# A routed mixture-of-experts layer: row numbers written by ScalarE, other banks for turned x, and the second tile's rows turned behind layer 2 of the first

## The chip, the cores and the metric

One core of one Trainium2 chip runs the whole kernel. The metric is the device time of one execution in microseconds (us); below, a time "at 24.77" is counted from the start of the profiled span.

The engines are PE (TensorE, with PEld for its weight loads), DVE (VectorE), ACT (ScalarE), POOL (GpSimd) and SP (which here only issues DMAs). Each works through its own queue in order. PE writes only to PSUM, which has eight banks, PB[0] to PB[7] in the code; ACT and DVE copy from there to SBUF.

## What is computed

Each of 4096 tokens (64 x 64) has 256 features. A gate, computed on the normalised token plus a term from its condition vector, picks 2 of 8 experts; every expert is a three-layer perceptron, and the two outputs are added to the token with the softmax weights of the two.

```
var = mean(x * x); xn = rms_w * (x * rsqrt(var + EPS))
gate = xn @ wg_W + wg_b + (cond @ gg_W + gg_b);  gate_w = softmax(gate)
topk_w, topk_i = top_k(gate_w, 2);  cw = one_hot(topk_i) weighted by topk_w, summed
h1 = relu(x @ W1[e] + b1[e]);  h2 = relu(h1 @ W2[e] + b2[e])
out = x + sum over e of cw[e] * (h2 @ W3[e] + b3[e])
```

W1 is 256 x 512, W2 512 x 512 and W3 512 x 256 for each expert, all in fp32.

## The kernel before

The kernel computes only the chosen experts. A **tile** is 128 tokens of one expert. Its rows are gathered from DRAM by an indirect DMA of POOL (`gather`, L719), turned by PE and copied by ACT into xT (`transpose_x`, L746), and taken through layer1 (L816), layer2 (L829) and layer3 (L846); then DVE scales the sum and POOL adds it into the output rows by another indirect DMA (`give`, L855). For each of the four column blocks of layer1 and layer2, PE accumulates into bank PB[0], PB[1], PB[2] or PB[3], and ACT applies the relu behind it.

The order within each engine is written out by hand: the whole body is under a manual schedule, so an engine's queue is the program's order of calls.

**The head of the program.** The first eight tiles, one of each expert, hold tokens of a first part of x alone (8 of the 32 rows of each partition), so that they can start before the rest has been routed.

- `first_part` (L398) loads x, squares it (`squares`, L180), turns it by PE (`turn_pe`, L192), copies it out of a bank (`turn_copy`, L202, by DVE or ACT; the row of the profile is L205 or L207), multiplies with the gate matrix (`gates_2`, L220; `gates`, L209), sets the result upright (`upright_2`, L227), chooses the experts (class `Part`, `choose`, L295), ranks the tokens, and finds the token of every slot of the first tiles by comparing row numbers with ranks (L477 to L481). The row numbers, `iotx`, are 128 numbers, each 16 times over, in fp16; POOL writes them with one iota at L417.
- `second_part` (L508) goes on with the rest of x beside the first gather: five more groups are turned, three of them here. `turn(j, c, n, eng, bank)` says which engine copies, and which bank of the list TB, that is PB[0], PB[1], PB[2], PB[5], PB[4], holds the turned group. PB[0] and PB[1] are also banks of layer1. `transpose_x(0)` is among these calls.
- `third_part` (L527) stands behind layer1 of tile 0: the last group is turned, the remaining squares follow on DVE, a first set of gates is set upright, and the gates of the last two groups are computed into PB[7] and copied by ACT into gTs.
- `last_upright` (L536) sets those last gates upright from gTs (eight matmuls, L231) into PB[6], and ACT copies them into graw, which the routing of the rest (`rest`, L549, a generator that hands DVE work out between the tiles) reads on DVE at L299. `rest` also reuses the memory of gTs from L555 on.
- `head_step` (L888) orders one of the first tiles. For tile 0, layer2 is called with functions that it calls in between (L907): after its second column block `last_upright`, after its third `transpose_x(1)`, the rows of the second tile. So the order on PE is blocks 0 and 1, the last upright gates, block 2, the rows of tile 1, block 3; on ACT it is the relus of blocks 0 and 1, the copy of the gates, the relu of block 2, the copy of xT, the relu of block 3.

After the first eight tiles come pairs of tiles and single tiles, in which PE has work without a break. The weights of all experts are loaded once, by DMAs that SP issues in one long row (`other_loads`, L489).

Of the kernel before, what the change touches and what calls it, by code (L numbers as in the profile page):

```python
# [21 lines left out]
def kernel(  # L22
# [17 lines left out]
    nc = tc.nc  # L40
# [40 lines left out]
    def buf(pool, shape, name, dt=F32):  # L81
        return pool.tile(shape, dt, tag=name, name=name)
# [91 lines left out]
    graw = t3("graw", NI)  # L174
    gTs = buf(gx, [P, TPB * P], "gTs")
    ohA = buf(gx, [P, P, GC], "hotA", F16)
    sqs = {"A": buf(gx, [P, H], "sqA", F16), "V": buf(gx, [P, H], "sqV", F16)}
    TB = [PB[k] for k in (0, 1, 2, 5, 4)]

# [7 lines left out]
    def turn(j, c, n, eng, bank):  # L187

        turn_pe(j, c, bank)
        turn_copy(n, eng, bank)  # L190
# [36 lines left out]
    def upright_2(dst):  # L227

        gtp = dst[:, 0 : TPB * P // 2].rearrange("p (k r) -> p k r", k=TPB)
        for k in range(TPB):  # L230
            nc.tensor.matmul(gtp[:, k], lhsT=gTs[:, ts(k, P)], rhs=both, start=True, stop=True)  # L231
        return gtp.rearrange("p k (q e) -> p q k e", q=2)[:, :, :, 0:E]

    def upright():

        gtp = PB[4].rearrange("p (k r) -> p k r", k=TPB)
        for k in range(TPB):
            nc.tensor.transpose(gtp[:, k], gTs[:, ts(k, P)], ident)
        return gtp.rearrange("p k (q e) -> p q k e", q=TPB)[:, :, :, 0:E]

    def busy(n):

# [155 lines left out]
    def first_part():  # L398


        rw2 = gTs[0:HC, 0:P]
        load_x(0)
        nc.scalar.dma_start(wg_in, wg_W.rearrange("(c p) e -> p c e", p=P))
        load_x(1)
        nc.scalar.dma_start(rw2, rms_w.rearrange("(c p) -> c p", c=HC))
        load_x(2, 2)
        nc.scalar.dma_start(gg_sb[0:G, :], gg_W)
        load_x(4, 2)
        nc.scalar.sqrt(warm, ones[:, 0:E])
        V.memset(wg_sb, 0.0)  # L410
        V.memset(condT[G : G + 2, :, :], 1.0)
        V.memset(cw8B, 0.0)
        for k in range(3):
            V.memset(ring(run, [P, H], "xg", 3, k), 0.0)
        V.memset(cgR, 0.0)
        nc.gpsimd.dma_start(cwdA.rearrange("(p i) e -> p i e", p=P)[:, NA:NI, :], cw8B[:, NA:NI, :])
        nc.gpsimd.iota(iotx, [[1, P], [0, GC]], base=0, channel_multiplier=0, allow_small_or_imprecise_dtypes=True)  # L417
        busy(7)
        rwp, cps, gps = PB[7][:, P : P + HC], PB[7][0:G, 2 * P : 2 * P + B], PB[7][:, 3 * P : 3 * P + E]
        nc.tensor.transpose(rwp, rw2, ident[:HC, :HC])  # L420
        V.tensor_copy(rwT, rwp)
        for c in range(HC):
            V.tensor_scalar(wg_sb[:, c, 0:E], wg_in[:, c, :], rwT[:, c : c + 1], None, ALU.mult)
        for i in (2, 3):
            squares(i, "A")
        turn(0, 0, 0, "V", 0)
        turn(0, 1, 1, "A", 1)
        squares(0, "V")
        turn(1, 0, 2, "V", 2)
        squares(TPB + 2, "A")  # L430
        turn(1, 1, 3, "A", 3)
        squares(TPB + 3, "A")
        nc.tensor.transpose(cps, cond_sb, ident[:B, :B])
        for i in (1, TPB, TPB + 1):
            squares(i, "V")
        V.tensor_copy(condT[0:G], cps.unsqueeze(2).to_broadcast([G, B, REP]))
        for j in range(NG - GA, NG):
            load_x(j)
        nc.sync.dma_start(vecs[0 : E * MC, :], b1.rearrange("e (c p) -> (e c) p", p=P))
        nc.sync.dma_start(vecs[E * MC : 2 * E * MC, :], b2.rearrange("e (c p) -> (e c) p", p=P))  # L440
        load_weights(0, (0, 1))
        gates_2(((0, 1), (2, 3)), PB[3])
        nc.scalar.copy(gTs, PB[3])
        pA.norm(True)
        turn(GA, 0, 0, "A", 0)
        nc.tensor.matmul(gps, lhsT=condT.rearrange("g b r -> g (b r)"), rhs=gg_sb, start=True, stop=True)
        V.tensor_copy(ggate, gps)
        chosen = pA.choose(upright_2(PB[4]))
        for q in (1, 2, 3):
            turn(GA + q, 0, q, "A", q)  # L450
        turn_pe(GA, 1, 0)
        next(chosen)
        turn_pe(GA + 1, 1, 4)
        for _ in chosen:
            pass
        pA.ranks()
        V.tensor_tensor(
            mvA.rearrange("p (k i) e -> p k i e", k=TOPK),
            pA.ohe.rearrange("p k e i -> p k i e"),
            toka.unsqueeze(1).unsqueeze(3).to_broadcast([P, TOPK, NA, E]),  # L460
            ALU.mult,
        )
        pA.exps()
        gates(0, range(4))
        turn_pe(GA + 2, 1, 1)
        turn_copy(0, "A", 0)
        turn_copy(1, "A", 4)
        turn_copy(2, "A", 1)
        V.scalar_tensor_tensor(
            pA.slot, pA.inc[:, 1:].rearrange("p (e i) -> p e i", e=E), -1.0, pA.along(pA.adj), ALU.add, ALU.add  # L470
        )
        pA.pick(lo16A.rearrange("p (k i) -> p k i", k=TOPK))
        tabA = PB[7][:, 0:E]
        GH = GC // 4
        for g0 in range(0, GC, GH):
            hs = slice(g0, g0 + GH)
            V.tensor_tensor(  # L477
                ohA[:, :, hs], iotx[:, :, hs], lo16A[:, hs].unsqueeze(1).to_broadcast([P, P, GH]), ALU.is_equal
            )
            for g in range(g0, g0 + GH):  # L480
                nc.tensor.matmul(tabA, lhsT=ohA[:, :, g], rhs=mvA[:, g, :], start=(g == 0), stop=(g == GC - 1))  # L481
        pA.totals()
        turn(GA + 3, 1, 3, "A", 2)

        V.tensor_scalar(sa[:, 0:E], tabA, 0.0, float(NT), ALU.is_equal, ALU.mult)
        V.scalar_tensor_tensor(idxA, tabA, float(OFFA), sa[:, 0:E], ALU.add, ALU.add)
        V.tensor_copy(totA1, pA.tot)
# [20 lines left out]
    def second_part():  # L508

        j0 = GA + 4  # L510
        vps = PB[6][:, 384 : 384 + 2 * E * MC]
        pA.weights()
        some(1)
        nc.tensor.transpose(vps, vecs, ident[: 2 * E * MC, : 2 * E * MC])
        V.tensor_copy(vT.rearrange("p l e c -> p (l e c)"), vps)
        some(1)
        turn(j0, 0, 4, "V", 3)
        some(2)
        turn(j0 + 1, 0, 6, "V", 0)
        gates(1, range(4))  # L520
        some(2)
        transpose_x(0)
        nc.scalar.copy(gTs, PB[3])
        turn(j0, 1, 5, "V", 1)
        some(4)

    def third_part():  # L527
# [8 lines left out]
    def last_upright():  # L536
        nc.scalar.copy(
            graw[:, NA + 4 * TPB : NI, :].rearrange("p (q k) e -> p q k e", q=2), upright_2(PB[6])
        )
# [289 lines left out]
    def layer2(u, between=None):  # L829
        _, bb, w2 = ww[u][0:3]  # L830
        w = len(tiles(u))
        for n in range(MC):
            ph = PB[n][:, 2 * BT : (2 + w) * BT]
            for m in range(MC):
                nc.tensor.matmul(  # L835
                    ph, lhsT=w2[:, m, ts(n, P)], rhs=hids[:, 0, m, 0 : w * BT], start=(m == 0), stop=(m == MC - 1)
                )
            nc.scalar.activation(hids[:, 1, n, 0 : w * BT], ph, AF.Relu, bias=bb[:, 1, n : n + 1])  # L838
            if between and n in between:
                between[n]()  # L840
# [47 lines left out]
    def head_step(u, more):  # L888

        if u + 3 < E:  # L890
            gather(u + 3)
        for k in range(3 * u, min(3 * u + 3, E)):
            gather_cw(k)
        table(GC * max(0, 2 * u - 9))
        layer1(u)
        if u == 0:
            third_part()
        else:
            transpose_x(u + 1)
            stage_1(u + 1)  # L900
            if u != 2:
                more(3200)
            scaled(u - 1, "A")
            layer3(u - 1)
        table(GC * max(0, 2 * u - 8))
        if u == 0:
            layer2(u, {1: last_upright, 2: lambda: transpose_x(1)})  # L907
            stage_1(1)
            more(3200)
        elif u == 2:  # L910
            layer2(u, {1: lambda: more(3200)})
        else:
            more(3200)
            layer2(u)
        if u >= 1:
            give(u - 1)

        if u >= E - 1 - NF:
            i = NA + (u - (E - 1 - NF)) * (NB // NF)
            fill = nc.sync.dma_start(our[:, i : i + NB // NF, :], xr[:, i : i + NB // NF, :])  # L920
            for a in adds:
                tc.declare_no_dep(fill.ins, a.ins, reason="the first E tiles hold tokens of the first part alone")
            fills.append(fill)
# [127 lines left out]
```

## Time and profile before

| what | us |
|---|---|
| median of three timed runs | 516.52 (516.45 to 517.2) |
| the profiled execution | 517.82 |
| its span | 516.1 |
| its time outside the span | 1.7 |
| PE busy | 498.1 |
| POOL busy | 292.7 |
| DVE busy | 240.5 |
| ACT busy | 164.3 |
| PE's idle time between 20 and 45 | 4.2 |

The busy time of PE is the sum of its matmuls as the profile models them; they overlap, so a busy PE is not a PE at its peak. A row of the timeline gives start, duration, engine, line, operation and tiles, with the number of instructions merged; in brackets stands how long the engine had been idle before it, and what ended that: "[0.71 <-DVE big L205]" is 0.71 us, ended by the DVE instruction of line 205 that writes the tile big. "issue" is a wait for which the profile shows no end, "remote" one whose semaphore was updated by something that it cannot name. The granted clock is given as a share of the full TensorE clock.

### The profile page before, as it was taken

Reading aid. Unit: us, or ns where it says so; the run is one execution under the profiler, and the core shown is the slowest. Engines: PE = TensorE matmul, PEld = TensorE weight load, DVE = VectorE, ACT = ScalarE, POOL = GpSimd, SP = SyncE. Lnnn points to the kernel's source line nnn. Section 1 sums busy time; section 2 is a strip of 40 time slices with the busy share of each in tenths; the row PEclk is TensorE's granted clock in tenths of the full one; section 3 lists DMA queues with packets and bytes.
Section 4 is the critical chain, followed back from the end, with each engine's and each line's share of the span. In section 5 each row is a group of like instructions: output and inputs, shape, how many; then the busy total and the mean of one; then the engine's idle time right before and its main releaser. Section 6 shows DMA issues by size and latency. Waiting matters only on the chain. (4 is left out here: it accounts for less than half of the span.)

```text
span 516.1 us, 8665 instructions
## 1 busy us (share of the span) xinstructions
PE 498.1 (97%) x2840; PEld 446.8 (87%) x2840; DVE 240.5 (47%) x589; ACT 164.3 (32%) x390; POOL 292.7 (57%) x229
## 2 busy tenths in 40 slices
PE   7879999999999999999999999999999999999992
PEld 6569999988888888888888888888888889999991
DVE  6883995444334333333444444334333336555550
ACT  4524534322222222222222222222222223443340
POOL 5464244886656656656565666655656545764621
PEclk9998999999999999999999999999999999999997
DMA  8599995444434343334344433334343242433201
GB/s 330 198 377 390 390 387 145 87 109 84 90 72 80 72 80 72 73 67 85 72 83 82 83 78 69 79 76 78 74 82 72 44 82 51 93 59 78 41 4 23
DMA packets 68257, 59.26 MB, mean 115 GB/s; under 512 B 39615, under 2 KB 59298, under 8 KB 67812
## 3 DMA queue, kind: packets, MB, share of 16 engines
q1 hardware_dynamic: 52608, 41.21, 24.6%
q0 software_dynamic: 15232, 17.34, 20.8%
q8 instruction: 25, 0.41, 0.3%
q14 instruction: 36, 0.29, 0.2%
q10 hardware_dynamic: 356, 0.01, 0.0%
HBM read 42.80 MB, written 20.71 MB: 123 GB/s over the span
## 5 line engine op out<-in xcount | busy, mean ns | idle before, releaser
L835 PE MATMUL pb<-hid,big 128*128 128x256 f32 (+1 forms) x1120 | 210.8, 346 | 0.0
L835 PEld LDWEIGHTS pb<-hid,big 128*128 128x128 f32 x1120 | 187.0, 191 | 20.4
L861 POOL DMA_INDIRECT out_dram<-y,idxR x59 | 97.8, 1658 | 127.1 <-issue 73.0
L838 ACT ACTIVATE hid<-pb,bb 128x256 f32<-128x256 f32 (+1 forms) x140 | 61.7, 441 | 245.3 <-PE pb L835 237.7
L790 DVE COPY big<-w2a 128x2048 f32 x35 | 44.3, 1266 | 160.6 <-PE pb L835 155.0
L824 PE MATMUL pb<-xT,big 128*128 128x256 f32 (+1 forms) x560 | 108.2, 346 | 0.0
L851 PE MATMUL pb<-big,hid 128*128 128x256 f32 x472 | 107.6, 379 | 0.0
L824 PEld LDWEIGHTS pb<-xT,big 128*128 128x128 f32 x560 | 93.5, 191 | 9.9
L851 PEld LDWEIGHTS pb<-big,hid 128*128 128x128 f32 x472 | 88.8, 190 | 11.6
L705 POOL DMA_INDIRECT big<-in_x_dram,idxR x59 | 79.5, 1348 | 20.7 <-issue 16.5
L705 POOL DMA_INDIRECT cg<-cwdR,idxR x59 | 69.2, 1172 | 18.0 <-issue 17.7
L827 ACT ACTIVATE hid<-pb,bb 128x256 f32<-128x256 f32 (+1 forms) x140 | 61.2, 441 | 41.4 <-PE pb L824 25.3
L860 DVE SCALAR_TENSOR_TENSOR y<-pb,cw,bc 128x256 f32<-128x256 f32 x59 | 28.5, 483 | 46.2 <-issue 25.1
L785 DVE COPY big<-w1a 128x1024 f32 x35 | 24.3, 694 | 26.2 <-PE pb L824 23.3
L861 POOL DMA_INDIRECT out_dram<-y,idxA x8 | 16.1, 2019 | 29.2 <-DVE denB L364 7.9
L835 PEld LDWEIGHTS pb<-hid,w2a 128*128 128x128 f32 x256 | 30.6, 195 | 1.2 <-ACT graw L532 0.8
L835 PE MATMUL pb<-hid,w2a 128*128 128x128 f32 x256 | 31.2, 279 | 0.0
L794 DVE COPY big<-w3a 128x1024 f32 x35 | 25.7, 735 | 2.9 <-issue 2.9
L809 DVE TENSOR_SCALAR bc<-b_sb,cw 128x256 f32 x59 | 23.0, 390 | 2.2 <-DVE cw L806 0.2
L749 DVE STREAM_TRANSPOSE xT<-gTs 128x256 f32<-128x256 f32 x57 | 22.5, 425 | 1.1 <-DMA gTs<-scr 1.1
L838 ACT ACTIVATE hid<-pb,vT 128x128 f32<-128x128 f32 x32 | 11.8, 368 | 29.4 <-PE pb L835 22.6
L824 PE MATMUL pb<-xT,w1a 128*128 128x128 f32 x128 | 16.5, 279 | 3.4 <-issue 2.7
(222 smaller groups left out, 259.8 us busy)
## 6 DMA issues: line engine op xcount, KB each, us to landing
w2a<-in_L_cond_W_dram SPq DMA_DIRECT2D x8, 1024.0 KB
scr<-big SPq DMA_DIRECT2D x57, 128.0 KB
gTs<-scr SPq DMA_DIRECT2D x228, 32.0 KB
w1a<-in_L_cond_W_dram SPq DMA_DIRECT2D x8, 512.0 KB
w3a<-in_L_cond_W_dram SPq DMA_DIRECT2D x8, 512.0 KB
out_dram<-in_x_dram SPq DMA_DIRECT2D x4, 768.0 KB
big<-in_x_dram SPq DMA_DIRECT2D x4, 512.0 KB
big<-in_x_dram SPq DMA_DIRECT2D x2, 1024.0 KB
```

The costliest lines, as they stand in the source:

```text
L705: return nc.gpsimd.indirect_dma_start(out=dst, out_offset=None, in_=src, in_offset=bass.IndirectOffsetOnAxis(ap=index(b), axis=0), bounds_ ...
L785: V.tensor_copy(st1, w1a[:, e].rearrange("p e c m -> p (e c) m"))
L790: V.tensor_copy(st2, w2a[:, ex[u]].rearrange("p e c m -> p (e c) m"))
L794: V.tensor_copy(st3, w3a[:, ex[u]].rearrange("p e c m -> p (e c) m"))
L809: V.tensor_scalar(bc, b3e, cw, None, ALU.mult)
L824: nc.tensor.matmul(ph, lhsT=w1[:, c, ts(m, P)], rhs=cols[:, c, :], start=(c == 0), stop=(c == HC - 1))
L827: nc.scalar.activation(hids[:, 0, m, 0 : w * BT], ph, AF.Relu, bias=bb[:, 0, m : m + 1])
L835: nc.tensor.matmul(ph, lhsT=w2[:, m, ts(n, P)], rhs=hids[:, 0, m, 0 : w * BT], start=(m == 0), stop=(m == MC - 1))
L838: nc.scalar.activation(hids[:, 1, n, 0 : w * BT], ph, AF.Relu, bias=bb[:, 1, n : n + 1])
L851: nc.tensor.matmul(po, lhsT=hids[:, 1, n, ts(k, BT)], rhs=w3[:, n, :], start=(n == 0), stop=(n == MC - 1))
L860: V.scalar_tensor_tensor(y, sums(b), cw, bc, ALU.mult, ALU.add)
L861: add = nc.gpsimd.indirect_dma_start(out=orows, out_offset=bass.IndirectOffsetOnAxis(ap=index(b), axis=0), in_=y, in_offset=None, bounds_c ...
```

## The change

Four edits, all in the head of the program.

1. The row numbers: POOL now writes 128 numbers once, in fp32, into memory that ohA uses later; ACT copies them out to iotx, each 16 times, in two halves of 64 numbers. The first half stands on ACT's queue behind the copy of the first turned group of the second part of x, the second half ahead of the two exponentials of the first part. The iota at L417 goes.
2. Two of the turned groups in `second_part` are copied by ACT instead of DVE.
3. The third of them goes through TB[3], that is PB[5], instead of TB[1], that is PB[1].
4. layer2 of tile 0 is called without functions in between; `transpose_x(1)` follows its last block, and `last_upright` follows that.

```diff
     ohA = buf(gx, [P, P, GC], "hotA", F16)
+    iotr = ohA.rearrange("p r g -> p (r g)")[:, 0 : 2 * P].bitcast(F32)
+    nc.gpsimd.iota(iotr, [[1, P]], base=0, channel_multiplier=0, allow_small_or_imprecise_dtypes=True)
...
+    def row_numbers(half):
+        hs = ts(half, P // 2)
+        nc.scalar.copy(iotx[:, hs], iotr[:, hs].unsqueeze(2).to_broadcast([P, P // 2, GC]))
...
-        nc.gpsimd.iota(iotx, [[1, P], [0, GC]], base=0, channel_multiplier=0, allow_small_or_imprecise_dtypes=True)
         busy(7)
...
         V.tensor_copy(ggate, gps)
+        row_numbers(0)
         chosen = pA.choose(upright_2(PB[4]))
...
+        row_numbers(1)
         pA.exps()
         gates(0, range(4))
...
-        turn(j0, 0, 4, "V", 3)
+        turn(j0, 0, 4, "A", 3)
         some(2)
-        turn(j0 + 1, 0, 6, "V", 0)
+        turn(j0 + 1, 0, 6, "A", 0)
         gates(1, range(4))
         some(2)
         transpose_x(0)
         nc.scalar.copy(gTs, PB[3])
-        turn(j0, 1, 5, "V", 1)
+        turn(j0, 1, 5, "V", 3)
         some(4)
...
         if u == 0:
-            layer2(u, {1: last_upright, 2: lambda: transpose_x(1)})
+            layer2(u)
+            transpose_x(1)
+            last_upright()
             stage_1(1)
             more(3200)
```

## The prediction, made before the changed kernel ran

> **What bounds the kernel now.** I read the page's busy times first, then PE's waits, then the timeline of PE, ACT, DVE and POOL up to 100 us. PE is busy for 97% of the span.
>
> ```profile
> PE 498.1 (97%) x2840; PEld 446.8 (87%) x2840; DVE 240.5 (47%) x589; ACT 164.3 (32%) x390; POOL 292.7 (57%) x229
> ```
>
> PE's waits over the whole span show none over 0.15 us after 38 us. So a microsecond that PE wins in the head shortens the span by as much, as long as nothing else is late behind it. The edits touch these rows of PE:
>
> ```profile
> 23.35 0.71 PE L824 MATMUL pb<-xT,w1a 128*128 128x128 f32 x4
> 24.77 1.60 PE L824 MATMUL pb<-xT,w1a 128*128 128x128 f32 x12 [0.71 <-DVE big L205]
> 26.21 0.60 PE L194 MATMUL pb<-ident,big 128*128 128x128 f32 x4
> ...
> 30.46 1.00 PE L231 MATMUL pb<-both,gTs 128*128 128x64 f32 x8
> 31.30 1.11 PE L835 MATMUL pb<-hid,w2a 128*128 128x128 f32 x8
> 32.25 0.40 PE L760 MATMUL pb<-ident,xg 128*128 128x128 f32 x2
> 32.48 1.06 PE L835 MATMUL pb<-hid,w2a 128*128 128x128 f32 x8
> 34.15 1.60 PE L824 MATMUL pb<-xT,w1a 128*128 128x128 f32 x12 [0.61 <-issue]
> 37.84 0.71 PE L824 MATMUL pb<-xT,w1a 128*128 128x128 f32 x4 [2.08 <-issue]
> ```
>
> Layer1 of tile 0 stops after its first block, because DVE's copy of a turned group (24.02 to 24.71) still holds PB[1]. Before layer1 of tile 1 PE waits for xT, whose copy sits in ACT's queue among the relus; the 2.08 us inside that layer1 are a third stop. ACT's side of it:
>
> ```profile
> 33.72 0.37 ACT L761 COPY xT<-pb 128x256 f32<-128x256 f32 x1 [0.34 <-PE pb L835]
> 37.41 0.37 ACT L838 ACTIVATE hid<-pb,vT 128x128 f32<-128x128 f32 x1 [3.32 <-remote]
> 40.34 1.14 ACT L827 ACTIVATE hid<-pb,vT 128x128 f32<-128x128 f32 x4 [2.56 <-remote]
> ```
>
> The relu at 37.41 needs matmuls that ended at 33.54, those at 40.34 need matmuls that ended from 34.86 on: PE's releases reached ACT up to 5 us late, a thing that the trace shows and doesn't explain. PE waits for the relu at 37.41 (both use PB[3]), and behind that idle time its clock drops:
>
> ```profile
> 38.00:40.00 2.00, 2.00 (x11) 1.77 (x12) 1.88 (x4) 0.00 (x0) 1.87 (x2) 0.79 1.02 378
> 40.00:42.00 2.00, 2.00 (x8) 1.64 (x7) 1.90 (x4) 1.66 (x6) 0.04 (x1) 0.50 1.12 422
> 42.00:44.00 2.00, 2.00 (x17) 2.00 (x17) 1.45 (x6) 0.52 (x2) 0.48 (x1) 0.86 0.98 402
> ```
>
> (The column behind the five engines is the granted clock.) At 0.79, 0.50 and 0.86 the three stretches lose 0.42 + 1.00 + 0.28 = 1.7 us.
>
> **The change part by part.**
>
> *Bank of the third turned group.* Layer1 without a stop takes 1.78 us of PE's queue (16 matmuls, 45.59 to the next row at 47.37; 0.111 each) and 0.11 to fill when PE was idle before. Here it took from 23.35 to 26.21, 2.86. **Gain 2.86 - 1.78 - 0.11 = 0.97.** What is late next: the group now needs PB[5], which ACT empties by about 20.8 and DVE by 24.06 (PE ends turning it at 23.33, the copy is 0.69). PE wants PB[5] again at 26.21 - 0.97 = 25.24, so 1.2 us are left. DVE then does four squares at 0.47 (20.20 to 20.67 is one step), to 25.94, and the copy of the last group can start at 25.84 + 0.1; it ends at 26.63, where 27.54 - 0.97 = 26.57 would keep PE's old pace. Cost below 0.1.
>
> *Two copies from DVE to ACT.* Each was 0.69 on DVE (L205) and is 0.59 on ACT (L207). ACT is idle from 20.09 to 22.93; PE ends turning the two groups at 20.20 and 20.64, so both are out by 21.5. Cost 0 under that cover. DVE wins 1.38, which is what lets it copy at once above. Without that cover they would push the xT copy of 22.93, one for one.
>
> *Order behind layer2 of tile 0.* Now layer2 starts at 28.57 and layer1 of tile 1 at 34.15: 5.58. After: 32 matmuls are 3.57 (64.65 to 68.22), the turn 0.23 (32.25 to 32.48), the upright gates 0.84 (30.46 to 31.30), the fill 0.11: 4.75. **Gain 0.83.** Is xT there? With layer2 from 27.60, its last matmul ends near 31.45, the relu (0.37) runs to 31.85, the xT copy (0.37) to 32.22; PE leaves the upright gates at 32.35. So they just cover the copy, by 0.1; without that cover the wait is back, up to 0.61 as now. graw is there at 32.9; DVE reads it (L299) at 37.23, or 1 us earlier now. L555 on DVE (34.48) must now wait for the upright matmuls to read gTs, to 32.65, about when DVE arrives. POOL's next gather into the second tile's buffer (34.19) waits for the turn, which comes at 31.3 instead of 32.25. Nothing new waits.
>
> *Row numbers.* Two ACT copies of 128x1024. The nearest rows are PSUM copies: 128x256 in 0.37, 128x512 in 0.59, so 0.86 ns an element and 1.03 each; I take that. Ends: not below 0.59 (half the elements), not above 2.49 (POOL's iota of all 2048). The places:
>
> ```profile
> 12.53 1.56 ACT L207 COPY hid<-pb 128x512 f32<-128x512 f32 x3 [1.11 <-PE pb L194]
> 14.11 1.28 ACT L357 ACT_TABLE_LOAD   x1
> 15.40 0.26 ACT L357 ACTIVATE wA<-wA 128x64 f32<-128x64 f32 x1
> ...
> 16.73 1.57 ACT L207 COPY hid<-pb 128x512 f32<-128x512 f32 x3 [0.97 <-PE pb L212]
> ```
>
> The first fills the idle 1.11; the second ends at 15.1 and pushes the copies of 16.73 by 0.06, ahead of another 1.20 idle at 19.50. DVE wants iotx at 16.76 (L477): in time. **Cost 0.** At 2.49 each the second would end at 18.0, 1.25 late for L477, and with it the first gather (19.39) and tile 0: the upper end, 1.25.
>
> *The iota that goes.* POOL wins 2.3 (2.49 less one like iot's 0.20), and had nothing to do before 12.98. Beside it DVE was held:
>
> ```profile
> 5.36 2.49 POOL L417 IOTA iotx<- 128x2048 f16 x1
> 5.96 1.93 DVE L205 COPY hid<-pb 128x512 f32<-128x512 f32 x1
> 7.67 0.69 DVE L205 COPY hid<-pb 128x512 f32<-128x512 f32 x1
> ```
>
> The same copy takes 1.93 beside the iota and 0.69 after it. But DVE's next copy, at 7.67, starts when PE ends its turn, and the gates wait at 9.16 for ACT's copy (8.52 to 9.11). **Gain 0**, at most the 0.42 that PEld waits there. [...]
>
> *Sum:* 0.97 + 0.83 = 1.8. The profiled execution is 516.1 + 1.72 outside its span = 517.82, and would be 516.0. The median of the timed runs lies 1.30 below it; I keep that distance: **514.7**. I leave the late releases as they are: either the timed runs don't have them, or they cost the same after.
>
> After 45 us weights are no limit: the trace has their landings 7 us or more ahead of use (w1a of tile 3 landed at 46.25, used at 53.58), so 1.8 earlier is safe.
>
> **The rivals.**
>
> *The late releases vanish.* They come while POOL issues seven gathers in a row (30.1 to 39.4) and PE runs 128-column matmuls; moved against that, they may miss. PE would also win 2.25 (37.84 against an unstopped 35.59) and 1.7 of clock, to 510.8; only the clock: 513.0. Against: POOL's burst starts with the landing at 29.34, which the change doesn't move. 0.17.
>
> *The late releases strike elsewhere* (slower). Tile 1 then runs layer1 at 32.35 to 34.13 and layer3 of tile 0 to 36.09, and layer2 waits for relus. If ACT gets them at 40.34 as now, PE idles until 40.76, 4.7 us, where now it is at full pace with a loss of 0.53 from 41.50, as from 42.03. At half clock until 42.57 it loses 0.9: 41.66, 516.2, about the same. At half clock for another 3.4 us it loses 2.6: 43.4, slower by 1.3, **517.9**. It decides when PE, released behind 39.9, has 1.7 or more to lose to the clock. [...] Chances: 0.14 slower, 0.07 same.
>
> *The rows of tile 8 are late.* POOL's gathers (85.31, 86.90) stand behind an add (83.44) that waited in its queue until the add before had landed at 82.66. They landed at 88.17 and 89.70; PE turns them at 90.59 and 90.70. If the landing doesn't move with PE, 1.0 is the most that can be won: 515.5, the same. For it: DMA is full until 82; against: that chain of adds starts with DVE work that PE's ranks (51.1) release, so it moves along. 0.12.
>
> *The change doesn't do what it says*: xT is late behind the relu, or the row numbers cost near their upper end: half the gain or less, 516.0. 0.04.
>
> **How the numbers follow.** Forecast 514.7 with 0.46. A measurement here can tell 0.2%, 1.03 us, from no change: faster is below 515.5. Faster 0.46 + 0.17 = 0.63; same 0.07 + 0.12 + 0.04 = 0.23; slower 0.14. The range runs from 512.8 (only the clock is won back, and a little) to 517.9; it leaves out the far end of the first rival, some 0.12, and a worse clock.
>
> **What would show it.** No stop inside L824 at 24; L824 of tile 1 at 32.3 to 32.4 right behind L231; ACT's two new rows near 1.0 us, ahead of 12.6 and of the table load; L477 still at 16.8 and L760 at 22.4; L760 of tile 8 near 88.8 without a wait. I am wrong if PE waits for ACT between 33 and 41 by another amount than now, if L477 moves, or if a stop opens near 89.

## The result, and the profile after

The changed kernel takes **517.05 us** (median of 20 runs, 513.2 to 519.03), the kernel before 516.59 (20 runs beside them, 514.16 to 517.9). The ratio is 0.9998, with a 95% interval of 0.9979 to 1.0017: no difference that can be measured, where 514.7 was forecast. The changed kernel's profiled execution took 513.2 (span 511.4), 4.6 less than the profiled execution before. So the trace has the gain and the median doesn't, and the question is where it goes.

First the trace. The timeline of PE in the changed kernel:

```profile
22.97 2.05 PE L831 MATMUL pb<-xT,w1a 128*128 128x128 f32 x16
24.86 0.60 PE L196 MATMUL pb<-ident,big 128*128 128x128 f32 x4
...
27.22 3.84 PE L842 MATMUL pb<-hid,w2a 128*128 128x128 f32 x32
...
31.97 2.00 PE L831 MATMUL pb<-xT,w1a 128*128 128x128 f32 x16
...
37.72 3.17 PE L842 MATMUL pb<-hid,w2a 128*128 128x128 f32 x26 [0.95 <-issue]
```

(L831, L842, L858, L767 and L233 are the lines that were L824, L835, L851, L760 and L231.) Layer1 of tile 0 has no stop: from its start to the next row it takes 24.86 - 22.97 = 1.89 us, where it took 2.86, so **0.97** less. From layer2 of tile 0 to layer1 of tile 1 it is 31.97 - 27.22 = 4.75, where it was 5.58, **0.83** less. The stop of 2.08 within layer1 of tile 1 has become one of 0.95 in layer2 of tile 1. No stretch at half clock is left between 10 and 500 us. With 0.38 by which the head happened to be earlier at 22 us, this makes 0.97 + 0.83 + 1.13 + 1.7 + 0.38 = 5.0; 4.7 of it is in the span.

ACT in the changed kernel:

```profile
10.91 1.05 ACT L245 CAST iotx<-hotA 128x1024 f16<-128x1024 f32 x1
...
40.29 1.14 ACT L845 ACTIVATE hid<-pb,vT 128x128 f32<-128x128 f32 x4 [1.95 <-PE pb L842]
```

The row numbers took 1.05 and, at 13.57, 1.07, and were in time. The last row is what remains wrong: four relus of layer2 start in one go at 40.29, though PE had ended the first of their matmul groups some 2 us before. PE's releases (the semaphore updates by which the other engines learn that a matmul is done) are late again, by up to 1.6 us: they bunch up (seven between 40.09 and 40.45) and the last late one comes out at 40.4, a microsecond after the last of seven gathers in a row on POOL:

```profile
30.07 1.06 POOL L712 DMA_INDIRECT cg<-cwdA,idxA  x1 [3.62 <-DMA cwdA<-cw8A]
...
38.32 1.00 POOL L712 DMA_INDIRECT cg<-cwdA,idxA  x1 [0.31 <-issue]
```

The updates of ACT and DVE in the same stretch aren't late: between 30 and 41 each comes 0.01 us behind the end of its instruction.

**The runs by their granted clock.** Every run has a mean granted clock, and in the profiled executions it tells how many stretches of 3.413 us at half clock (granted 0.50; in the kernel before from 39.16 to 42.57) lie between 10 and 500 us: none at 0.992 to 0.995, one at 0.989 to 0.991, two (or one twice as long) at 0.987 to 0.988. The number of runs in each class, with the class's median in us behind it, is:

| kernel | median | 0.992 and over | 0.989 to 0.991 | 0.988 and under |
|---|---|---|---|---|
| before (all 78 runs beside the experiments) | 516.9 | 43: 516.8 | 35: 517.0 | 0 |
| after | 517.05 | 8: 513.8 | 5: 517.1 | 7: 518.7 |

The changed kernel has runs near the forecast and below it, eight of 20. Twelve lose 3.3 to 4.9 us, and by this measure seven have two stretches at half clock, which the kernel before never had. By my estimate from the granted 0.50, one stretch at half clock costs at most 3.413 / 2 = 1.7 us; the rest must lie elsewhere, in waits or in a later start (in the 14 profiles of this document, layer1 of tile 0 starts between 22.40 and 24.78). The class doesn't settle the time: the 35 runs of the kernel before with one stretch are two groups, 13 at 514.2 to 514.8 and 22 at 516.8 to 518.9, with none between.

My theory after this: *both gains are real, and the late releases give them back.* They come with POOL's row of seven gathers; what PE wins ahead of them moves its waits to another place, and the idle time also costs clock. The rivals: the late releases have another cause (the big copy from DRAM to DRAM that runs at that time, or POOL being busy with anything); one of the two edits costs something that the trace of one execution doesn't show; the clock falls for reasons that have nothing to do with PE's waits.

### The profile page after: what moved, and what is told of

Its sections match the earlier page's. It is cut to its first block, busy times and chain, and to the rows that moved or that the text cites. A ratio compares the mean times of both kernels' runs of the same rounds, so it can differ in the third digit from the quotient of the medians.

```text
span 511.4 us, 8669 instructions
## 1 busy us (share of the span) xinstructions
PE 495.6 (97%) x2840; PEld 445.4 (87%) x2840; DVE 239.2 (47%) x587; ACT 167.3 (33%) x394; POOL 288.9 (56%) x229
## 5 line engine op out<-in xcount | busy, mean ns | idle before, releaser
L842 PE MATMUL pb<-hid,big 128*128 128x256 f32 (+1 forms) x1120 | 210.8, 346 | 0.0
L842 PEld LDWEIGHTS pb<-hid,big 128*128 128x128 f32 x1120 | 187.0, 191 | 20.4
L831 PE MATMUL pb<-xT,big 128*128 128x256 f32 (+1 forms) x560 | 108.2, 346 | 0.0
L858 PE MATMUL pb<-big,hid 128*128 128x256 f32 x472 | 107.6, 379 | 0.0
L831 PEld LDWEIGHTS pb<-xT,big 128*128 128x128 f32 x560 | 93.5, 191 | 9.9
L858 PEld LDWEIGHTS pb<-big,hid 128*128 128x128 f32 x472 | 88.8, 190 | 11.6
L842 PEld LDWEIGHTS pb<-hid,w2a 128*128 128x128 f32 x256 | 29.9, 192 | 2.3 <-issue 2.0
L842 PE MATMUL pb<-hid,w2a 128*128 128x128 f32 x256 | 30.7, 277 | 0.9 <-issue 0.9
L831 PE MATMUL pb<-xT,w1a 128*128 128x128 f32 x128 | 16.0, 278 | 0.0
```

The costliest lines, as they stand in the source:

```text
L831: nc.tensor.matmul(ph, lhsT=w1[:, c, ts(m, P)], rhs=cols[:, c, :], start=(c == 0), stop=(c == HC - 1))
L842: nc.tensor.matmul(ph, lhsT=w2[:, m, ts(n, P)], rhs=hids[:, 0, m, 0 : w * BT], start=(m == 0), stop=(m == MC - 1))
L858: nc.tensor.matmul(po, lhsT=hids[:, 1, n, ts(k, BT)], rhs=w3[:, n, :], start=(n == 0), stop=(n == MC - 1))
```

## The experiments

### One edit at a time

`e1_banks` is the kernel before with the three lines of edits 2 and 3:

```diff
-        turn(j0, 0, 4, "V", 3)
+        turn(j0, 0, 4, "A", 3)
...
-        turn(j0 + 1, 0, 6, "V", 0)
+        turn(j0 + 1, 0, 6, "A", 0)
...
-        turn(j0, 1, 5, "V", 1)
+        turn(j0, 1, 5, "V", 3)
```

> Edits 2 and 3 alone (two copies by ACT, the third group through PB[5]). Both theories expect the stop inside layer1 of tile 0 (0.71 in the profile of before) to be gone and everything to about 32 us to come 0.9 to 1.0 earlier. If each microsecond of PE counts (the sum of the prediction): 515.6 where before is 516.6. If the late releases between 32.4 and 40.3 end at a fixed time, set by what POOL or the DMA queues do, the gain is swallowed there: layer2 of tile 1 still starts near 41 and the median stays within 0.5 of before, with single runs some us apart by the granted clock.

Measured: 517.6 us (12 runs), ratio 1.0002 (0.997 to 1.0034). Its timeline of PE, and then two stretches of its windows (length, then busy time and count of PE, PEld, DVE, ACT, POOL, granted clock, DMA share, GB/s):

```profile
32.41 1.97 PE L824 MATMUL pb<-xT,w1a 128*128 128x128 f32 x16
...
38.17 0.49 PE L835 MATMUL pb<-hid,w2a 128*128 128x128 f32 x2 [1.38 <-issue]
39.68 2.71 PE L835 MATMUL pb<-hid,w2a 128*128 128x128 f32 x11 [1.02 <-issue]
```

```profile
36.19:39.60 3.41, 1.10 (x7) 0.71 (x5) 3.12 (x7) 0.71 (x3) 2.80 (x3) 1.00 1.02 391
39.60:43.01 3.41, 3.33 (x15) 3.33 (x16) 2.89 (x8) 1.43 (x5) 1.15 (x3) 0.50 1.07 410
```

Two things are to be seen. Layer1 of tile 1 starts at 32.41 **without a wait, in the old order**, 4.80 behind layer2 of tile 0 (27.61): the wait that the order edit was to remove is already gone. And the microsecond won is given back at once: PE waits 1.38 and 1.02 in layer2 of tile 1, is busy for 1.10 of one stretch, and gets half clock in the next.

`e2_order` is the kernel before with edit 4 alone:

```diff
-            layer2(u, {1: last_upright, 2: lambda: transpose_x(1)})
+            layer2(u)
+            transpose_x(1)
+            last_upright()
```

> Edit 4 alone (rows of tile 1 turned behind layer2 of tile 0, the last upright gates behind them). The stop of 0.61 ahead of layer1 of tile 1 goes, layer1 of tile 1 starts 0.8 earlier. By the sum 515.8 where before is 516.6. With late releases that end at a fixed time: within 0.5 of before, and the wait moves from inside layer1 of tile 1 to layer2 of tile 1, as in the changed kernel.

Measured: 517.65 us (12 runs), ratio 1.0025 (1.0001 to 1.005), so nothing won. Its PE:

```profile
33.21 2.05 PE L824 MATMUL pb<-xT,w1a 128*128 128x128 f32 x16 [0.63 <-issue]
...
39.81 2.45 PE L835 MATMUL pb<-hid,w2a 128*128 128x128 f32 x13 [2.58 <-ACT hid L827]
```

With the new order alone the wait in front of layer1 of tile 1 is **still there**, 0.63. So it wasn't the order that made it; it is the first of the late releases (PE had turned the rows of tile 1 by 31.74, and ACT's copy of them starts at 32.79, on a release of PE), and by these two kernels it depends on whether PE gets there before they begin. The 2.58 behind it is the next one, and half clock follows from 40.82 here too (0.50 to 44.24).

### What makes the releases late

`e4_fill_later` moves the big copy from DRAM to DRAM behind the load of the third set of weights, in the changed kernel:

```diff
-        fills.append(nc.sync.dma_start(our[:, 0:NA, :], xr[:, 0:NA, :]))
         load_weights(2)
+        fills.append(nc.sync.dma_start(our[:, 0:NA, :], xr[:, 0:NA, :]))
```

> The changed kernel with the copy of the first output rows (DRAM to DRAM, 1 MB) issued behind the weights of expert 2 instead of ahead of them, so that it runs some 5 us later. If that copy holds PE's releases back: the late releases start and end some 5 us later or vanish between 33 and 37, and the time changes with them. If POOL's row of gathers does: late releases at 32.4 to 40.3 as before, runs from 513 to 519, median within 1 of the changed kernel's 517.

Measured: 518.71 us (12 runs), ratio 1.0035 (1.0018 to 1.0053). The releases are late in the same stretch, and PE stands idle longer:

```profile
37.40 0.49 PE L842 MATMUL pb<-hid,w2a 128*128 128x128 f32 x2 [1.67 <-issue]
40.29 1.95 PE L842 MATMUL pb<-hid,w2a 128*128 128x128 f32 x9 [2.40 <-ACT hid L834]
```

The copy was issued at 29.09 in place of 24.95, but the late updates end with the seventh gather as before (gather to 38.8, last late update at 40.1; in the changed kernel 39.3 and 40.4). The copy isn't the cause. The median is 1.7 above the changed kernel's, more than the 1 that I had expected. This profile also shows a run of the changed kernel's order at its worst: 4.07 us of waits, and half clock (0.50) from 41.19 to 44.60.

`e3_cw_spread` is the changed kernel with one gather of gate weights a step in place of three, so that POOL issues a row of three gathers there and not of seven:

```diff
-        for k in range(3 * u, min(3 * u + 3, E)):
+        for k in range(u, E if u == E - 2 else u + 1):
             gather_cw(k)
```

> The changed kernel with one gather of gate weights in each of the first tiles' steps instead of three in every third step, so that POOL issues three indirect gathers in a row behind 30 us where it issued seven. If POOL's row of gathers is what holds PE's releases back: the late releases end some 5 us earlier (near 35 instead of 40.3), PE has no wait over 0.3 between 33 and 41, no run has a low clock there, and the runs lie near 512.5 to 514 with little scatter. If the DMA queues (weights, the copy of the first rows) or chance hold them back: late releases up to 40.3 again, runs from 513 to 519 as in the changed kernel, median near 517.

Measured: **513.44 us** (9 runs, 512.8 to 514.26), ratio 0.9934 (0.9912 to 0.9955), every run at 0.993 or over. POOL and PE in its timeline:

```profile
31.49 1.23 POOL L712 DMA_INDIRECT cg<-cwdA,idxA  x1 [3.43 <-DMA cwdA<-cw8A]
33.15 1.00 POOL L712 DMA_INDIRECT xg<-in_x_dram,idxA  x1 [0.43 <-PE pb L767]
34.45 1.00 POOL L712 DMA_INDIRECT cg<-cwdA,idxA  x1 [0.30 <-issue]
```

```profile
37.36 3.73 PE L842 MATMUL pb<-hid,w2a 128*128 128x128 f32 x32
```

The row of gathers ends at 35.5 and layer2 of tile 1 runs in one piece. No update of PE is over 0.3 us late (up to 1.6 in the changed kernel's profile, counted from the matmul that ended last).

Two kernels ask what about the row does it. `e11_gathers_back` keeps this spreading and adds four gathers that nothing reads; `e10_pool_iota` adds, at the same place, eight iotas that nothing reads.

```diff
             gather_cw(k)
+        if u == 1:
+            for k in range(4):
+                fetch(extra[:, k], cwdA[:, :], k)
```

> The changed kernel with spread gathers, and with four further gathers of gate weights into a tile that nothing reads, behind the second step's own, so that GpSimd again issues seven in a row, from 30 to about 40 us, while every gather that is used stays where the spreading put it. Theory (the length of the row of gathers makes PE's releases late): the late releases are back, with waits in layer 2 of the second tile and low clocks in many runs: 516.5 to 517.5 us. Rival (the spreading gained because some needed gather came at a better time, not because the row was shorter): as without the four, about 513.5 us.

Measured: 518.19 us (12 runs), ratio 1.0033 (1.0008 to 1.0059). The late updates are back (up to 1.7 us behind the last matmul), with them 0.19 and 1.05 us of waits in layer2 of tile 1, and only four of 12 runs at 0.992 or over. Those four have 515.8, 2.4 more than e3 without the four gathers. Part of the loss lies elsewhere: at 88 us this profile has another 3.7 us of waits for the rows of tiles 8 and 9, which the four gathers don't explain, and its half clock, 0.50 from 90.03 to 96.86, stands behind these and not behind the late updates.

```diff
             gather_cw(k)
+        if u == 1:
+            for k in range(8):
+                nc.gpsimd.iota(sqs["V"], [[1, H]], base=k, channel_multiplier=0, allow_small_or_imprecise_dtypes=True)
```

> The changed kernel with spread gathers, and with eight iota instructions into a dead scratch tile put behind the second step's gate-weight gather, about 0.65 us each, so that GpSimd is busy from 34.5 to about 40 us as in the changed kernel, but not with gathers. Theory (the late releases come with the row of indirect gathers, not with GpSimd being busy): as without the iotas, about 513.5 us, PE's releases no more than 0.3 us late. Rival (any busy GpSimd makes them late): 516 to 517.5 us, with releases up to 5 us late until the iotas end and a wait of over 0.9 us in layer 2 of the second tile.

Measured: 514.22 us (12 runs), ratio 0.9967 (0.994 to 0.9995), ten of 12 runs at 0.992 or over with 514.0. The iotas took 3.26 us and not the 5.2 that I had planned, so POOL was busy to 37.4 and not to 40; within that stretch no update is over 0.31 late and PE doesn't wait. A POOL that is busy without gathers doesn't bring it, as far as 3.26 us show. The other two runs, at 0.987, took 518.5 and 518.6; what they lost isn't shown by any profile (the one of this kernel has 2.9 us of waits for the rows of tiles 8 and 9, without half clock).

### The edits without late releases

Four kernels with the spread gathers, on one chip: the kernel before (`e5_before_spread`), with edits 2 and 3 (`e6_banks_spread`), with edit 4 (`e7_order_spread`), and the changed kernel, the same as e3 (`e8_after_spread`). The edits are those shown above.

> The kernel before, with the gate weights' gathers issued one per step instead of three at a time, so that GpSimd issues no row of seven gathers beside layers 1 and 2. Theory (the change is worth its 1.8 us of stops, and the late releases that GpSimd's row of gathers brings took it back): no late releases, but the stop in layer 1 of the first tile and the order of the second tile's rows are as before, so 513.4 (the changed kernel with this spreading, in the last comparison) + 1.8 = about 515.2 us, 1.4 under the kernel before. Rival A (the spreading alone is worth the whole 3.4 us, the change nothing): about 513.4 us. Rival B (the spreading helps only with the changed order): about 516.5 us. The trace should show the stop of about 0.8 us within layer 1 of the first tile and no PE semaphore more than 0.3 us late.

> As the kernel before with spread gathers, and with the bank and copy edit alone (the turned x of the first tile in banks that are free, copied by ScalarE). Theory: the stop in layer 1 of the first tile is gone and nothing takes it back, so 515.2 - 0.97 = about 514.2 us. Rival A: as the kernel before with spread gathers, about 513.4 us. Rival B: about 516.5 us, or the gap of 0.97 us is found again as a wait further on.

> As the kernel before with spread gathers, and with the order edit alone (the second tile's rows turned behind layer 2 of the first, the last upright gates behind them). Theory: the wait in front of layer 1 of the second tile is gone and nothing takes it back, so 515.2 - 0.83 = about 514.4 us. Rival A: as the kernel before with spread gathers, about 513.4 us. Rival B: about 516.5 us.

> The changed kernel with spread gathers once more, on the same chip as the three others: 513.4 us expected by all. Theory: it lies 1.8 us under the kernel before with spread gathers, and the two single edits with spread gathers lie between, their gains adding up (0.97 + 0.83), which leaves about 0 for the row numbers moved to ScalarE. Rival A: all four kernels with spread gathers agree within 0.5 us.

| kernel with spread gathers | median | ratio to before (95%) | 0.992 and over | 0.989 to 0.991 | 0.988 and under |
|---|---|---|---|---|---|
| as before | 516.9 | 1.0007 (0.998 to 1.0034) | 4: 515.1 | 4: 517.5 | 4: 518.5 |
| banks and copies | 512.97 | 0.9917 (0.9898 to 0.9935) | 5: 512.9 | 1: 516.8 | 0 |
| order | 515.99 | 0.9996 (0.9972 to 1.0019) | 6: 515.3 | 5: 518.6 | 1: 518.2 |
| all of the change | 513.57 | 0.9931 (0.9904 to 0.9957) | 5: 513.5 | 1: 516.3 | 0 |

The theory's numbers hold for the last kernel alone. The medians of the first and the third lie near rival B's 516.5, that of the second under all three. Spreading alone brings the kernel before nothing in the median (516.9 against 516.61 beside it). In the medians the whole change is worth 516.9 - 513.57 = 3.3 us; among the runs without half clock it is 515.1 - 513.5 = 1.6, near the theory's 1.8. But it doesn't split as expected. Among those runs banks and copies are worth 2.2 and the order nothing: with it the times are 0.2 higher without the other edits, and 0.6 higher, the row numbers included, on top of them. The trace says why the order is worth nothing. PE in the kernel before with spread gathers:

```profile
24.43 2.69 PE L824 MATMUL pb<-xT,w1a 128*128 128x128 f32 x12 [0.77 <-DVE big L205]
...
34.53 1.95 PE L824 MATMUL pb<-xT,w1a 128*128 128x128 f32 x16
```

Layer1 of tile 1, at 34.53, has no wait, in the old order: 4.80 behind the start of layer2 of tile 0 (29.73), against 4.75 in the new order. Without late releases the order edit wins 0.05 us.

In eight of 12 runs the kernel before with spread gathers has half clock all the same, although nothing is late. The same profile shows where, and the one with the order edit shows the same two stops without it:

```profile
21.32:24.73 3.41, 1.95 (x12) 1.52 (x13) 3.06 (x12) 1.23 (x3) 2.71 (x6) 1.00 0.53 125
24.73:28.14 3.41, 3.41 (x18) 3.41 (x17) 1.43 (x7) 1.10 (x3) 1.48 (x2) 0.50 0.82 309
```

```profile
19.72:23.13 3.41, 2.72 (x22) 1.64 (x22) 3.04 (x13) 0.64 (x2) 3.00 (x5) 1.00 0.24 68
23.13:26.55 3.42, 2.62 (x21) 2.19 (x20) 3.15 (x13) 1.85 (x5) 2.52 (x4) 1.00 0.71 226
```

In both kernels PE waits about 0.7 for the rows of tile 0 and then 0.8 inside layer1. In the traces the granted clock keeps its value for whole stretches of 3.413 us, counted from its first rise. In the profile of the kernel before it rises at 8.44, is 0.50 from 39.16, nine stretches later, to 42.57, and falls again at 510.20, 147 stretches behind the rise; in the changed kernel's it rises at 7.52 and falls at 505.87, 146 stretches later; in the first profile above the two stretches at half clock begin at 24.73 and 89.58, 19 stretches apart. The rise lies between 6.7 and 11.2 us in the 14 profiles. In the first kernel both stops fell into one stretch (busy 1.95) and the next ran at half clock, where layer1's remaining rows took 2.69 (1.60 in the second); in the second the border fell between them. So the stop that the bank edit removes costs its 0.8 us, and where both stops fall into one stretch, as in the first profile, up to 1.7 us of clock behind it by the estimate above. With the stop gone, 2 of the 12 runs of the two kernels without it were under 0.992; with it, 14 of 24.

### Filling PE's wait

`e9_fill_idle` puts matmuls that nothing reads into layer2 of tile 1 of the changed kernel, to keep PE busy while it waits:

```diff
             for m in range(MC):
+                for _ in range(4 if u == 1 and n == 0 else 0):
+                    nc.tensor.matmul(PB[3][:, BT : 2 * BT], lhsT=w2[:, m, ts(0, P)], rhs=w2[:, m, ts(1, P)], start=True, stop=True)
                 nc.tensor.matmul(
```

> The changed kernel with 16 further matmuls in layer 2 of the second tile, four ahead of each of the first four, which nothing reads (left over in a free part of a bank, 0.13 us each, 2.05 us together). They depend on nothing that is late, so they run where TensorE would wait for the late relus of layer 1; when the relus come doesn't change. Theory (in the ten profiles taken so far each 3.413 us stretch at half clock follows a stretch of the same length and grid in which TensorE was busy under about 2.0 us; the late releases make such a stretch, and it costs 1.7 us): in nearly all runs the mean granted clock is 0.992 to 0.995 and none of the times above 518 that the changed kernel has at 0.987 remains; the wait itself stays, and where there is none the matmuls cost up to 2.05 us, so the median is about 515.2 us, 1.8 under the changed kernel's 517.05. Rival (the granted clock falls for another reason and TensorE's waits don't decide it): clocks of 0.987 to 0.990 as often as before, and a median of 517 to 519 us.

Measured: 524.28 us (6 runs), ratio 1.0157 (1.0123 to 1.019), no run over 0.990. This is a miss, and the kernel a poor test. Each such matmul is two instructions (four of them are a row of eight, 1.06 us), so the filling cost 4 x 1.06 = 4.2 us and not 2.05.

```profile
35.92 2.05 PE L831 MATMUL pb<-xT,w1a 128*128 128x128 f32 x16 [1.15 <-ACT xT L768]
```

This row of PE shows that the wait which was to be filled had moved: 1.15 in front of layer1 of tile 1, ahead of the filling (39.77). The stretch at half clock of this profile is at 20.62, behind a stretch in which PE was busy for 3.25 us, 1.4 of them with matmuls of 8 columns. All profiles have these matmuls, but in no other does half clock follow so busy a stretch. What kept the clock low in the other runs isn't shown, so the rival isn't refuted: the granted clock was low in all six runs.

### A better spreading

`e12_pairs` is the changed kernel with one gather in each of the first two steps and two in the next three, because the first spreading leaves two to be issued in front of the rows of tiles 8 to 11, for which PE then waited (0.31 and 0.75 us at 86 in the changed kernel with spread gathers):

```diff
-        for k in range(3 * u, min(3 * u + 3, E)):
+        for k in [[0], [1], [2, 3], [4, 5], [6, 7], [], []][u]:
             gather_cw(k)
```

> The changed kernel with another spreading of the gate weights' gathers: one in each of the first two steps, then two, two and two, so that none is left to be issued in front of the rows of tiles 8 to 11, for which TensorE waited 0.6 to 2.4 us around 87 us in the spread kernels, with half clock behind it in two of their five profiles. Theory: those waits go, and with them the runs at 0.990: 0.3 to 1.0 us under the first spreading, so about 512.8 us, and all runs between 511.9 and 514.5. Rival (three gathers in a row in the later steps bring late releases of their own): 513.5 to 515 us.

Measured: **512.64 us** (6 runs, 511.87 to 513.6), ratio 0.9932 (0.9906 to 0.9958), all runs at 0.992 or over. Layer2 of tile 1 runs from 36.22 in one piece, and PE's turning of the rows of tiles 8 and 9 at 85.67 has no wait. It beats the kernel before by 4.3 us and the changed kernel by 4.4; against the first spreading the difference is too small for these runs to settle.

## Why the forecast failed, though its range held

The measured 517.05 lies inside the stated range, 512.8 to 517.9, but that is owed to the range's upper end, which a rival had set, and not to the sum: the forecast was 514.7, with 0.63 for faster and 0.23 for the same. The sign of being wrong that the prediction named, PE waiting for ACT between 33 and 41 by another amount than now, came up in the trace: 0.95 in place of 0.61 and 2.08.

1. *Bank of the third turned group, gain 0.97.* Right: 0.97 in the trace. Its worth to the time is larger, 2.2 between runs without half clock; the trace accounts for 1.04 of that (layer1 of tile 0 with its row behind: 2.93 with the order edit alone, 1.89 with the bank edit, both with spread gathers), and the rest isn't located.
2. *Two copies from DVE to ACT, cost 0.* Right: the copies took 0.58 each at 20.36 and 21.31. The second stood 0.36 behind an instruction of DVE and was out at 21.9 instead of by 21.5, still 0.65 before the copy of xT (22.54).
3. *Order behind layer2 of tile 0, "Gain 0.83".* The 0.83 stands in the trace to the digit, and it isn't the order's. The bank edit alone removes the wait (e1), the order alone doesn't (e2: 0.63), and without late releases it isn't there in either order. I took a wait that the late releases made for one that the queue of ACT made. The row that I had in hand said "issue" and not ACT.
4. *Row numbers, cost 0.* Right: 1.05 and 1.07 for the estimated 1.03. The consumer on DVE started at 16.44, earlier than before. Together with the order it measured 0.6 more than banks and copies alone, which these runs can't tell from nothing.
5. *The iota that goes, gain 0.* Right as far as the profiles tell: layer1 of tile 0 starts between 22.40 and 23.48 in the six profiles with the iota and between 22.77 and 24.78 in the eight without, so the 0.38 of the changed kernel's one profile is luck. I misread the row of 1.93, though. Ahead of that copy in DVE's queue stood the scaling of the gate matrix from SBUF (L423), which took 2.78 beside the iota and 0.37 in the changed kernel; it ended at 7.89, the iota at 7.85, and the copy out of PSUM behind it at 7.89 too.
6. ***"I leave the late releases as they are: either the timed runs don't have them, or they cost the same after." This is the step that failed.*** They don't stay as they are. In all seven profiles with the long row the last late update comes 0.7 to 1.3 us behind the end of POOL's seventh gather, whatever PE does, so what PE wins ahead of them it waits for behind them, in layer2 of tile 1 (0.95 in the changed kernel, 2.40 with the banks alone, 2.58 with the order alone, 4.07 in e4). That was my rival "the late releases strike elsewhere", which had 0.14 and 0.07; its place (layer2 of tile 1 waiting for relus), its price (half clock for another stretch) and its time (517.9) are near the 517.1 to 518.7 of twelve of the 20 runs. That the row of seven gathers brings it is shown by e3, e11 and e10; that half clock comes behind the waits is shown in the profiles of e1, e2 and e4 (PE busy for 1.10, 1.01 and 1.01 of the 3.413 us ahead of it), and only argued for the timed runs of the changed kernel, whose one profile has none.
7. *"The median of the timed runs lies 1.30 below it; I keep that distance."* This went with it: the changed kernel's profiled execution lies 3.85 below its median. One execution out of a spread of 5.8 us says little about the middle.
8. *The late releases vanish, 510.8.* With the gathers spread they do, at 512.6 to 513.6: nearer to the 513.0 that I gave the clock alone.
9. *The rows of tile 8 are late.* Not in the changed kernel's profile, where PE turns them at 85.82 without a wait. But in the kernels with the first spreading this rival came up: PE waits 0.6 to 2.4 us for these rows in e3 and e5 to e8.

Open: why a row of indirect gathers makes PE's updates late; where the second stretch at half clock lies in the changed kernel's runs at 0.987; and why a stretch at half clock hardly moves the kernel before (516.8 without, 517.0 with one). That its waits are there in either case would be a guess, and it doesn't explain the 13 runs at 514.2 to 514.8.

## What to carry to other kernels

Before pricing an edit, ask of every wait that it removes who ends it: a wait that the profile can't name a releaser for may belong to something else, and then it only moves. Where something holds an engine until a fixed time, gains ahead of it are worth nothing until that thing is removed, so try its removal first: here one line that spreads the gathers brought 3 to 4 us on top of the change and nothing without it, and only with that line did the bank edit pay. And judge such edits by many runs and their granted clocks: a profile of one execution showed 4.7 us that the median didn't have.

## What the runs showed of the hardware

- **PE's semaphore updates came late while POOL issued a long row of indirect gathers.** With seven in a row, 1.3 to 1.7 us apart, updates were late by up to 2.4 us behind the last matmul (1.7 in the kernel before, 1.6 in the changed one; relus by up to 5), in all seven profiles that have such a row between 30 and 41 us (in e1 by no more than 0.9). With three in a row they were at most 0.3 late, in six of six; 3.26 us of iotas behind the three don't change that. It isn't confined to this stretch: around 85 us, behind a row of an add and four gathers (e12), an update is 1.1 late, and in one of an add and six gathers (e3) 1.5. Why it happens isn't shown.
- **Half clock came behind stretches in which PE had stood idle in part.** In the 14 profiles, between the clock's first rise and 495 us, all six stretches of 3.413 us in which PE was busy under 1.4 us were followed by one at half clock (1.33 in the kernel before, 1.10 in e1, 1.01 in e2 and in e4, 1.35 in e6, 0.50 in e11), two of the six with 1.74 to 1.98 (1.95 and 1.75, both in e5), and none of the eleven with 2.05 to 2.60 (2.46 in the changed kernel). The stretch of 3.25 in e9 is the one exception; e11 had a second stretch at half clock behind one that ran at half clock itself. The idle time was one or two gaps in a stretch, none over 2.6 us (2.08 alone in the kernel before; 0.69 and 0.77 in e5).
- An ACT copy of 128x1024 elements from fp32 to fp16, its source read 16 times over by a broadcast, took 1.05 to 1.07 us; the estimate from the rows of PSUM copies (0.37 for 256, 0.59 for 512) was 1.03.
